# VectorE's signed step tied, by issue order, behind a residual sum written ahead of it

## The chip, the cores and the metric

The kernel runs on one core of a Trainium2 chip. The metric is the device time of one execution in microseconds (us), taken as the median of several runs. The profile shows five engines and the queues that issue DMAs: PE is TensorE (PEld its weight loads), DVE is VectorE, ACT is ScalarE, POOL is GpSimd, SP is SyncE, whose queue issues most transfers here.

## What is computed

Four layers run one after the other on x of 4 batches x 64 channels x 256 x 256 in float32. Layers 0, 1 and 3 are long convolutions with a filter that a small network produces; the filter is a product of a row part and a column part, so the two-dimensional convolution splits into two products with Toeplitz matrices:

```python
k_f = jnp.fft.rfft2(k, s=(fft_size, fft_size)) / fft_size
u_f = jnp.fft.rfft2(x.astype(jnp.float32), s=(fft_size, fft_size))
y = jnp.fft.irfft2(u_f * k_f, s=(fft_size, fft_size))[..., :L, :L]
out = y + x * bias[:, None, None]
```

Layer 2 is a Haar transform, a mixing of the channels with a soft threshold at each coefficient, twice, and the inverse transform:

```python
f1 = haar2d(x)
acc = jnp.zeros_like(f1[:, :conv_w.shape[1]])
for i in range(v.shape[0]):
    f3 = f1 * v[i]
    f4 = jnp.einsum('bchw,oc->bohw', f3, conv_w[i])
    f5 = jnp.sign(f4) * jax.nn.relu(jnp.abs(f4) - tau[i])
    acc = acc + f5
y = haar2d(acc, inverse=True)
return y + x
```

## The kernel before

The work is staged by batch. `convolutions(b)` takes the 64 channels of a batch through layers 0 and 1 and the forward Haar transform and stores the coefficients in DRAM. `mixing(b)` takes the coefficients back in 64 groups g, mixes the channels and thresholds. `inverse(b)` transforms back channel by channel and applies layer 3. While batch b is mixed, batch b + 1 is convolved; the last mixing (b = 3) has layer 3 of some put-off channels beside it instead.

One channel c of a convolution passes through these steps. PE multiplies the input with the layer's Toeplitz matrix into a PSUM bank (`pa0`), ACT copies it out (`a0`, L275), PE multiplies again (`py0`), and VectorE forms the residual sum `y0` = x * bias + py0 (L292, `residual`, shown as y<-x,bsb,py in the profile). That is the first layer. The second does the same from `y0` to `y1` (`pa1`, `a1`, `py1`, then y<-y,bsb,py). After it come `sums` and `sd` (L337, L338), levels of the transform (L350, L351), a split into two parts (`sp`, L369 on ACT, L374 on VectorE), a product on PE (`pz`) and a copy and store (`co`, L393).

One group g of a mixing passes through these: four products on PE into `px` (L449); a scaling of part of it on VectorE (L468) and of the rest on ACT, in up to 12 small steps (L473), both into the tile `f4`; `mag` = |f4| on ACT (L477); the sign of `f4`, in place, on ACT (L480); `shrink`, mag minus the threshold, on VectorE (L484); `signed`, max(mag, 0) times the sign, on VectorE (L488, shown as mag<-mag,f); and `add`, two additions into the large tile `z` (L494). The tiles `f4` and `mag` have two buffers each, and `px` two. The buffer of `f4` comes free after `signed`, that of `mag` after `add`, that of `px` after the ACT steps of L473. Level steps on `z` (`halve`, L299 and L300) undo the transform along one axis as soon as enough of `z` is there.

The order is made in two steps. First the program lists every stage of every unit with a time, counted in ticks, from the table `PLACE`, and writes the instructions in the order of these times. In the first three mixings `signed` of group g stands at tick g + 2.802, and the residual sum of a channel at its own tick + 2.571; 64 channels are spread over some 70 ticks. Then the scheduler of the framework, when it compiles, goes through the instructions in the written order as priority, and puts an instruction into its engine's queue when, by its reckoning, its inputs and a buffer are ready. So an instruction that is ready early can overtake what was written before it. After that each engine's order is fixed and every engine works its queue off in order. A dependency of the kind `order` (no synchronisation) ties one instruction behind another in the queue, and adds no semaphore wait.

```python
order = mybir.DependencyInfo(mybir.DependencyClass.NoSync, mybir.DependencyReason.DATA)
```

The kernel before uses it at a few places of its beginning, where the filters are made.

Of the kernel before, what the change touches and what calls it, by code (L numbers as in the profile page):

```python
# [12 lines left out]
ALU = mybir.AluOpType  # L13
# [3 lines left out]
B, C, S, EMB, ORD = 4, 64, 256, 33, 64  # L17
# [80 lines left out]
def conv_seq_kernel(ctx, tc, x, fz, fw, bias, decay, haar, haar_row, factors, vt, taut, wmix, out):  # L98
# [14 lines left out]
    nc = tc.nc  # L113
# [19 lines left out]
    bsb = const.tile([P, 3, C], F32, name="bsb")  # L133
# [24 lines left out]
    order = mybir.DependencyInfo(mybir.DependencyClass.NoSync, mybir.DependencyReason.DATA)  # L158
# [90 lines left out]
    def toeplitz(layer, c, name):  # L249

        t = tp.tile([P, 2, S], F32, name=name, tag="toep")
        nc.sync.dma_start(t, ap(pads[layer], c * 2 * ROW, [[1, P], [ROW, 2], [1, S]]))
        return t

    def bank(name):
        return psm.tile([P, 2, S], F32, name=name, tag="mm")

    def contract(ps, src, t):

        for m in range(2):  # L260
            nc.tensor.matmul(ps[:, m, :], src[:, 0, m * P : (m + 1) * P], t[:, ::-1], start=True, stop=False)  # L261
            nc.tensor.matmul(ps[:, m, P:], src[:, 1, m * P : (m + 1) * P], t[:, : P - 1 : -1], start=False, stop=True)  # L262
# [16 lines left out]
    def second(b, st, key, layer, res, new, tag, ahead=None):  # L279


        def product(c):
            s = st[c]
            if ahead is not None:
                s[ahead] = toeplitz(ahead, c, f"t{ahead}_{b}_{c}")
            s["p" + new] = bank(f"p{new}_{b}_{c}")
            contract(s["p" + new], s[key], s[layer][:, 1, :])

        def residual(c):
            s = st[c]  # L290
            y = io.tile([P, 2, S], F32, name=f"{new}_{b}_{c}", tag=tag, bufs=BUFS[tag])
            nc.vector.scalar_tensor_tensor(y, s[res], bsb[:, layer, c : c + 1], s["p" + new], ALU.mult, ALU.add)  # L292
            s[new] = y

        return [product, residual]

    def halve(even, odd):

        nc.vector.tensor_sub(odd, even, odd)  # L299
        nc.vector.scalar_tensor_tensor(even, even, 2.0, odd, ALU.mult, ALU.subtract)  # L300

    def level(n, chunk, begin=0, count=None):

        count = n if count is None else count
        v = z.rearrange("p n s x c -> p n s (x c)")[:, chunk].rearrange("p (j e s) x -> p j e s x", e=2, s=P // 2 // n)
        halve(v[:, begin : begin + count, 0, 0, :], v[:, begin : begin + count, 1, 0, :])

    def butterfly():

# [9 lines left out]
    def at(time, run, unit):  # L319
        events.append((time, len(events), run, unit))  # L320
# [104 lines left out]
    def mixing(b, start, n_act):  # L425

        st = {}

        def load(g):
            f = mx.tile([P, 2, S], F32, name=f"f_{b}_{g}", tag="f", bufs=3)  # L430
            nc.sync.dma_start(f, coef[b].rearrange("k c p w -> (k c) p w")[:, 2 * g : 2 * g + 2])
            st[g] = {"f": f}
            if g % GT == 0:
                t = mx.tile([P, 2, GT, 16], F32, name=f"vt_{b}_{g}", tag="vt")
                nc.sync.dma_start(t, scales[g // GT])
                st["vt", g // GT] = t

        def scale(g, i):
            return st["vt", g // GT][:, i, g % GT, :]

        def over(g, i, n):
            return scale(g, i)[:, :n].unsqueeze(2).to_broadcast([P, n, C])

        def mix(g):
            f = st[g]["f"]
            ps = psx.tile([P, 2, 2, S], F32, name=f"px_{b}_{g}", tag="mix")
            for q in range(2):
                for h in range(2):
                    nc.tensor.matmul(  # L449
                        ps[:, q, h, :],  # L450
                        f[:, q, h * P : (h + 1) * P],
                        wb.rearrange("p r n -> p (r n)"),
                        start=True,
                        stop=True,
                    )
            if g == 0:

                one, two = ps[:, 0, :, :P], ps[:, 0, :, P:]
                d = mx.tile([P, 2, P], F32, name=f"d_{b}", tag="mag")
                nc.vector.tensor_copy(d, two)  # L460
                nc.vector.tensor_sub(two, one, d)
                nc.vector.tensor_add(one, one, d)
            st[g]["f4"] = mx.tile([P, 16, C], F32, name=f"f4_{b}_{g}", tag="f4")
            st[g]["px"] = ps.rearrange("p q h (r i o) -> p (q h r i) o", r=2, i=2)

        def scaled(g):
            px, n = st[g]["px"], 16 - n_act
            nc.vector.tensor_tensor(st[g]["f4"][:, :n], px[:, :n], over(g, 0, n), ALU.mult)  # L468

        def scaled_too(g, half):  # L470
            px, f4 = st[g]["px"], st[g]["f4"]
            for j in range(16 - n_act + half * (n_act // 2), 16 - (1 - half) * (n_act - n_act // 2)):
                nc.scalar.mul(f4[:, j], px[:, j], scale(g, 0)[:, j : j + 1])  # L473

        def size(g):
            mag = st[g]["mag"] = mx.tile([P, 16, C], F32, name=f"mag_{b}_{g}", tag="mag")
            nc.scalar.activation(mag, st[g]["f4"], AF.Abs)  # L477

        def sign(g):
            nc.scalar.activation(st[g]["f4"], st[g]["f4"], AF.Sign)  # L480

        def shrink(g):
            mag = st[g]["mag"]
            nc.vector.tensor_sub(mag, mag, over(g, 1, 16))  # L484

        def signed(g):
            mag = st[g]["mag"]
            nc.vector.scalar_tensor_tensor(mag, mag, 0.0, st[g]["f4"], ALU.max, ALU.mult)  # L488

        def add(g):  # L490
            parts = st.pop(g)["mag"].rearrange("p (q x i) (n c) -> p q i x n c", q=2, i=2, n=4)
            for q in range(2):
                to = slot(2 * g + q)
                nc.vector.tensor_add(  # L494
                    z[:, :, to].rearrange("p n x c -> p x n c"), parts[:, q, 0], parts[:, q, 1]
                )


        for g in range(S // 4):
            for name, stage in zip(  # L500
                ("mix load", "mix", "scaled", "scaled too", "scaled rest", "size", "sign", "shrink", "signed", "add"),
                (
                    load,
                    mix,
                    scaled,
                    lambda g: scaled_too(g, 0),
                    lambda g: scaled_too(g, 1),
                    size,
                    sign,
                    shrink,  # L510
                    signed,
                    add,
                ),
            ):
                at(start + g + PLACE[name if b + 1 < B else "l " + name], stage, g)

    def inverse(b, start, put_off):

        st = {}
# [40 lines left out]
        def join(c):  # L560
            ps = st[c]["pw"]
            t = io.tile([P, 2, 2, P], F32, name=f"t_{b}_{c}", tag="res", bufs=BUFS["res"])
            nc.vector.scalar_tensor_tensor(t, st[c]["r"], 0.5, ps, ALU.mult, ALU.add)
            u = io.tile([P, 2, S], F32, name=f"u_{b}_{c}", tag="y", bufs=BUFS["y"])
            v = u.rearrange("p m (w e) -> p m w e", e=2)
            nc.vector.tensor_add(v[:, :, :, 0], t[:, 0], t[:, 1])
            nc.vector.tensor_sub(v[:, :, :, 1], t[:, 0], t[:, 1])
            st[c]["u"] = u
# [20 lines left out]
        for c in range(C):  # L589
            for name, stage in zip(("sooner", "early", "fetch", "rows"), (sooner, early, fetch, rows)):  # L590
                at(start + c + PLACE[name], stage, c)
            turn = start + c
            if c < 16:
                at(start + c + PLACE["halves"], halves, c)
                at(start + c + PLACE["cols"], cols, c)
                turn += 1
            at(turn + PLACE["join"], join, c)
            if c in put_off:
                at(turn + PLACE["aside"], aside, c)
            else:  # L600
                shift = (0.0, 0.0)
                if put_off:
                    shift = ((-0.27, -0.342), (0.23, 0.158))[c % 3]
                for name, stage in zip(("a3", "a3 copy", "y3", "y3 sum", "out"), last(b, st)):
                    at(turn + PLACE[name] + shift[name[0] != "a"], stage, c)
# [59 lines left out]
    ahead = C  # L665
    start = ready + 3
    for b in range(B):
# [11 lines left out]
        ahead = start - 3  # L679
# [4 lines left out]
def slot(i):  # L684

    if i == 0:
        return 0
    n = 1 << i.bit_length() - 1
    return (2 * (i - n) + 1) * (P // 2 // n)
# [104 lines left out]
```

## Time and profile before

| what | us |
|---|---|
| median of 3 runs | 2876.38 |
| lowest and highest | 2875.58 and 2878.57 |
| the profiled execution's own time | 2874.07 |
| its span in the profile | 2872.3 |
| mixing 0, with its beginning | 448 to 856 |
| mixing 1, with its beginning | 1064 to 1510 |
| mixing 2, with its beginning | 1714 to 2158 |
| last mixing | 2358 to 2640 |

The stages between these are the inverse transforms; the first 448 us are the filters and the first batch's convolutions. Times in the lines of a profile are counted from the start of the span. A busy table by stage has, in each row, the stretch and its length, then busy us and number of instructions of PE, PEld, DVE, ACT and POOL, the share of the granted TensorE clock, the share of the DMA engines and GB/s. A line of waits has the engine that waited and for which tile and line, what released it, and us in total, times, and the longest. A line of the timeline has the start, the us, the engine, the line, the operation, out<-in, and how many were merged.

### The profile page before, as it was taken

To read this page: it belongs to the slowest core of one execution; us is meant where nothing else is said; L and a number is where in the kernel's file an instruction comes from. 1 tells how busy PE (TensorE), PEld (TensorE's weight loads), DVE (VectorE), ACT (ScalarE), POOL (GpSimd) and SP (SyncE) were. 2 spreads that over 40 slices of the span, in tenths; PEclk is the share of its full clock that TensorE was granted. 3 is DMA by queue.
4 is the path that set the end of the run, shared out by engine and by line. 5 is a ranking of instruction groups with operands and counts; after the bars stand their busy time and mean duration, and the time that the engine had idled before them with its cause. 6 is when DMAs were issued, how large, how long until landed. Compare 5 with 4: busy or idle time off the path is not lost. (4 is left out here: it accounts for less than half of the span.)

```text
span 2872.3 us, 52434 instructions
## 1 busy us (share of the span) xinstructions
PE 2827.1 (98%) x16592; PEld 2555.6 (89%) x16592; DVE 2494.9 (87%) x4255; ACT 2080.3 (72%) x4950; POOL 334.4 (12%) x644
## 2 busy tenths in 40 slices
PE   9999999999999999999999999999999999999999
PEld 7899998898888898998898998998898998888998
DVE  4655558999999779999999779999999779999985
ACT  2333338999995558998985658999995659998554
POOL 0111111121121001221221001121121000000000
PEclk9999999999999999999999999999999999999999
DMA  6878787776667986777777986777777988787786
GB/s 182 249 231 230 232 232 227 207 208 204 205 209 213 289 254 198 214 213 214 209 207 236 299 255 196 213 214 216 208 208 235 297 266 235 229 238 212 224 241 201
DMA packets 599367, 649.77 MB, mean 226 GB/s; under 512 B 48465, under 2 KB 517044, under 8 KB 598964
## 3 DMA queue, kind: packets, MB, share of 16 engines
q1 hardware_dynamic: 536996, 578.61, 68.9%
q10 hardware_dynamic: 62096, 67.82, 6.7%
q8 instruction: 134, 2.20, 0.3%
q14 instruction: 141, 1.16, 0.1%
HBM read 426.77 MB, written 219.48 MB: 225 GB/s over the span
## 5 line engine op out<-in xcount | busy, mean ns | idle before, releaser
L261 PE MATMUL py<-t,a 128*128 128x256 f32 x3072 | 922.5, 382 | 9.5 <-ACT a L275 8.7
L275 ACT COPY a<-pa 128x512 f32<-128x512 f32 x768 | 478.8, 623 | 498.6 <-PE pa L262 455.2
L473 ACT ACTIVATE f<-px,vt 128x64 f32<-128x64 f32 x2816 | 610.5, 367 | 101.6 <-DVE f L468 101.1
L262 PEld LDWEIGHTS py<-t,a 128*128 128x128 f32 x3072 | 583.4, 190 | 79.3
L262 PE MATMUL py<-t,a 128*128 128x128 f32 x3072 | 590.0, 274 | 0.0
L261 PEld LDWEIGHTS py<-t,a 128*128 128x128 f32 x3072 | 497.3, 191 | 51.2 <-ACT a L275 19.0
L449 PE MATMUL px<-wb,f 128*128 128x256 f32 x2048 | 487.6, 380 | 7.6 <-ACT f L473 7.6
L449 PEld LDWEIGHTS px<-wb,f 128*128 128x128 f32 x2048 | 369.0, 190 | 50.0 <-ACT f L473 10.5
L351 POOL TENSOR_TENSOR sd<-less 128x128 f32<-128x128 f32 (+4 forms) x320 | 190.8, 596 | 1858.7 <-DVE less L350 1519.9
L534 ACT COPY zc<-z 128x512 f32<-128x512 f32 x256 | 282.1, 1105 | 108.1 <-PE pw L542 99.0
L484 DVE TENSOR_TENSOR mag<-mag,vt 128x1024 f32<-128x1024 f32 x256 | 316.6, 1237 | 12.3 <-ACT mag L477 11.5
L488 DVE SCALAR_TENSOR_TENSOR mag<-mag,f 128x1024 f32<-128x1024 f32 x256 | 316.6, 1238 | 0.0
L261 PE MATMUL pa<-t,y 128*128 128x256 f32 x1024 | 309.1, 384 | 6.8 <-DVE y L292 5.2
L261 PE MATMUL pa<-t,x 128*128 128x256 f32 x1024 | 305.9, 381 | 0.5 <-DMA t<-pad 0.5
L477 ACT ACTIVATE mag<-f 128x1024 f32<-128x1024 f32 x256 | 295.7, 1155 | 2.8 <-DVE z L494 0.4
L374 DVE TENSOR_TENSOR sp<-sd,sp 128x512 fp32r<-128x512 f32 x256 | 179.8, 702 | 129.3 <-ACT sp L369 128.2
L480 ACT ACTIVATE f<-f 128x1024 f32<-128x1024 f32 x256 | 285.8, 1116 | 3.5
L261 PE MATMUL pa<-t,u 128*128 128x256 f32 x772 | 233.2, 384 | 6.5 <-ACT w L548 2.8
L292 DVE SCALAR_TENSOR_TENSOR y<-x,bsb,py 128x512 f32<-128x512 f32 x256 | 190.9, 746 | 41.9 <-PE py L262 41.0
L262 PEld LDWEIGHTS pa<-t,x 128*128 128x128 f32 x1024 | 194.6, 190 | 26.3
L262 PEld LDWEIGHTS pa<-t,y 128*128 128x128 f32 x1024 | 194.5, 190 | 26.3
L292 DVE SCALAR_TENSOR_TENSOR y<-y,bsb,py 128x512 f32<-128x512 f32 x256 | 190.7, 745 | 26.0 <-PE py L262 25.6
(73 smaller groups left out, 4412.3 us busy)
## 6 DMA issues: line engine op xcount, KB each, us to landing
t<-pad SPq DMA_DIRECT2D x768, 256.0 KB, 4.1
x<-in_x SPq DMA_DIRECT2D x256, 256.0 KB, 3.7
coef<-co SPq DMA_DIRECT2D x256, 256.0 KB, 3.2
f<-coef SPq DMA_DIRECT2D x256, 256.0 KB, 3.2
r<-keep SPq DMA_DIRECT2D x256, 256.0 KB, 4.1
out_y<-y ACTq DMA_DIRECT2D x193, 256.0 KB, 4.3
keep<-sums SPq DMA_DIRECT2D x256, 128.0 KB, 2.8
keep<-sd SPq DMA_DIRECT2D x256, 128.0 KB, 2.8
```

What stands on the lines that cost most here:

```text
L261: nc.tensor.matmul(ps[:, m, :], src[:, 0, m * P : (m + 1) * P], t[:, ::-1], start=True, stop=False)
L262: nc.tensor.matmul(ps[:, m, P:], src[:, 1, m * P : (m + 1) * P], t[:, : P - 1 : -1], start=False, stop=True)
L275: nc.scalar.copy(a, s["p" + new])
L292: nc.vector.scalar_tensor_tensor(y, s[res], bsb[:, layer, c : c + 1], s["p" + new], ALU.mult, ALU.add)
L351: engine.tensor_tensor(t[:, :, :, half:length], v[..., 0], v[..., 1], ALU.subtract)
L449: nc.tensor.matmul(ps[:, q, h, :], f[:, q, h * P : (h + 1) * P], wb.rearrange("p r n -> p (r n)"), start=True, stop=True,)
L473: nc.scalar.mul(f4[:, j], px[:, j], scale(g, 0)[:, j : j + 1])
L477: nc.scalar.activation(mag, st[g]["f4"], AF.Abs)
L480: nc.scalar.activation(st[g]["f4"], st[g]["f4"], AF.Sign)
L484: nc.vector.tensor_sub(mag, mag, over(g, 1, 16))
L488: nc.vector.scalar_tensor_tensor(mag, mag, 0.0, st[g]["f4"], ALU.max, ALU.mult)
L534: nc.scalar.copy(a.rearrange("p h k i -> p (h k) i"), z[:, c // 16, :, :, c % 16].rearrange("p i x -> p x i"))
```

## The change

A variable `behind` holds the instruction that was written last among the residual sums of the first layer (`y0`) and the joins of the inverse transform (`join`, L563). In the first three mixings each `signed` step gets a dependency of the kind `order` on it. `halve` and `level` get a parameter `stay` with a dependency of the same kind, but no call sets it, so it has no effect.

```diff
+    behind = [None]
...
-            nc.vector.scalar_tensor_tensor(y, s[res], bsb[:, layer, c : c + 1], s["p" + new], ALU.mult, ALU.add)
+            done = nc.vector.scalar_tensor_tensor(y, s[res], bsb[:, layer, c : c + 1], s["p" + new], ALU.mult, ALU.add)
+            if new == "y0":
+                behind[0] = done
             s[new] = y
...
-    def halve(even, odd):
-
-        nc.vector.tensor_sub(odd, even, odd)
+    def halve(even, odd, stay=False):
+
+        first = nc.vector.tensor_sub(odd, even, odd)
+        if stay and behind[0] is not None:
+            tc.add_manual_dep(first.ins, behind[0].ins.name, order, reason="not ahead of the joins")
         nc.vector.scalar_tensor_tensor(even, even, 2.0, odd, ALU.mult, ALU.subtract)
...
         def signed(g):
             mag = st[g]["mag"]
-            nc.vector.scalar_tensor_tensor(mag, mag, 0.0, st[g]["f4"], ALU.max, ALU.mult)
+            step = nc.vector.scalar_tensor_tensor(mag, mag, 0.0, st[g]["f4"], ALU.max, ALU.mult)
+            if b + 1 < B and behind[0] is not None:
+                tc.add_manual_dep(step.ins, behind[0].ins.name, order, reason="the residual sum goes first")
...
         def join(c):
             ps = st[c]["pw"]
             t = io.tile([P, 2, 2, P], F32, name=f"t_{b}_{c}", tag="res", bufs=BUFS["res"])
-            nc.vector.scalar_tensor_tensor(t, st[c]["r"], 0.5, ps, ALU.mult, ALU.add)
+            behind[0] = nc.vector.scalar_tensor_tensor(t, st[c]["r"], 0.5, ps, ALU.mult, ALU.add)
```

More of the change, by code (lines that the diff above doesn't have):

```diff
@@ L291, in residual, with level @@
             y = io.tile([P, 2, S], F32, name=f"{new}_{b}_{c}", tag=tag, bufs=BUFS[tag])
-            nc.vector.scalar_tensor_tensor(y, s[res], bsb[:, layer, c : c + 1], s["p" + new], ALU.mult, ALU.add)
+            done = nc.vector.scalar_tensor_tensor(y, s[res], bsb[:, layer, c : c + 1], s["p" + new], ALU.mult, ALU.add)
+            if new == "y0":
+                behind[0] = done
             s[new] = y
         return [product, residual]
-    def halve(even, odd):
-        nc.vector.tensor_sub(odd, even, odd)
+    def halve(even, odd, stay=False):
+        first = nc.vector.tensor_sub(odd, even, odd)
+        if stay and behind[0] is not None:
+            tc.add_manual_dep(first.ins, behind[0].ins.name, order, reason="not ahead of the joins")
         nc.vector.scalar_tensor_tensor(even, even, 2.0, odd, ALU.mult, ALU.subtract)
-    def level(n, chunk, begin=0, count=None):
+    def level(n, chunk, begin=0, count=None, stay=False):
         count = n if count is None else count
         v = z.rearrange("p n s x c -> p n s (x c)")[:, chunk].rearrange("p (j e s) x -> p j e s x", e=2, s=P // 2 // n)
-        halve(v[:, begin : begin + count, 0, 0, :], v[:, begin : begin + count, 1, 0, :])
+        halve(v[:, begin : begin + count, 0, 0, :], v[:, begin : begin + count, 1, 0, :], stay)
     def butterfly():
```

## The prediction, made before the result was known

> **What bounds the kernel now.** I read the page's busy shares first, then busy time by stage, then what TensorE (PE) waited for in the mixings, then one tick on VectorE (DVE) and ScalarE (ACT).
>
> ```profile
> PE 2827.1 (98%) x16592; PEld 2555.6 (89%) x16592; DVE 2494.9 (87%) x4255; ACT 2080.3 (72%) x4950; POOL 334.4 (12%) x644
> ```
>
> PE is idle for 2872.3 - 2827.1 = 45.2 us of the whole span. The change touches only mixings 0 to 2, so the stages come next (start:end, length, then busy us by engine).
>
> ```profile
> 515.00:856.00 341.00, 335.37 (x1856) 299.02 (x1855) 336.13 (x551) 319.16 (x913) 70.69 (x107) 1.00 0.70 207
> 1130.00:1510.00 380.00, 378.70 (x2126) 341.01 (x2125) 376.71 (x613) 343.62 (x959) 77.87 (x120) 1.00 0.73 212
> ...
> 515.00:666.00 151.00, 149.69 (x828) 133.53 (x827) 149.52 (x248) 144.28 (x415) 29.36 (x47) 1.00 0.71 209
> 666.00:856.00 190.00, 185.67 (x1029) 165.49 (x1029) 186.61 (x304) 174.88 (x500) 41.32 (x60) 1.00 0.69 206
> ```
>
> In mixing 1 PE idles 1.30 of 380 us and DVE 3.29: PE sets the pace, DVE just keeps up. Mixing 2 is its copy (376.73 of 378). Mixing 0 idles 5.63 of 341, 4.33 of it in its second part. The starts of mixings 1 and 2 (66 us each) add 0.92 each and the start of mixing 0 0.06, so all PE idle in the three mixings is 5.69 + 2.22 + 2.19 = 10.1 us. What ended it, mixing 0 first, then mixing 1:
>
> ```profile
> PE py L261 <- ACT a L275: 3.1, 5, 1.4
> PE px L449 <- ACT f L473: 1.4, 2, 1.1
> PE pa L261 <- DVE y L292: 1.0, 3, 0.5
> ...
> PE pa L261 <- DVE y L292: 0.5, 3, 0.2
> PE py L261 <- ACT a L275: 0.5, 1, 0.5
> ```
>
> The residual sum is the smaller part; the copy `a` on ACT is the larger. Now a tick of mixing 1, DVE and then ACT:
>
> ```profile
> 1148.94 1.24 DVE L488 SCALAR_TENSOR_TENSOR mag<-mag,f 128x1024 f32<-128x1024 f32 x1
> 1150.07 0.77 DVE L292 SCALAR_TENSOR_TENSOR y<-x,bsb,py 128x512 f32<-128x512 f32 x1
> 1150.73 0.78 DVE L494 TENSOR_TENSOR z<-mag 128x256 f32<-128x256 f32 x2
> ```
>
> ```profile
> 1149.08 2.56 ACT L473 ACTIVATE f<-px,vt 128x64 f32<-128x64 f32 x12 [0.84 <-DVE f L468]
> 1151.45 0.67 ACT L275 COPY a<-pa 128x512 f32<-128x512 f32 x1
> ...
> 1152.91 1.17 ACT L477 ACTIVATE mag<-f 128x1024 f32<-128x1024 f32 x1
> 1154.11 1.06 ACT L480 ACTIVATE f<-f 128x1024 f32<-128x1024 f32 x1
> 1155.08 0.57 ACT L275 COPY a<-pa 128x512 f32<-128x512 f32 x1
> ```
>
> The reader is to see two things. VectorE's order is not the written order: the signed step at 1148.94 (group 11) runs ahead of the sum `y0` of channel 12 at 1150.07, and group 10's ran at 1141.9, though channel 12's sum is written ahead of both. And ACT has a queue in which `f`, `mag`, sign and the copies `a` stand behind each other.
>
> **The change part by part.** It adds and removes no instruction and no DMA: 192 signed steps (start to next start 1.13 us) stay, each tied by issue order alone. Matching the n-th instruction of each line in the trace with the n-th written, 180 of the 192 now run ahead of the sum they will be tied to (54, 63, 63 by mixing), always a `y0`, never a join. From a signed step's start now to the issue of what follows that sum is in the median 5.2 us in mixing 0 and 7.0 us in 1 and 2. So DVE's busy sum is unchanged, and the signed step moves by about one tick (7.4 us). SP's and POOL's queues hold nothing of it: the loads `f<-coef` wait for the mix matmuls, not for the signed step. What follows:
>
> *A, the sum comes earlier.* A signed step no longer stands just ahead of a `y0`. That is worth at most PE's waits on DVE `y` over the five windows of the three mixings, 1.0 + 0.9 + 0.5 + 0.9 + 0.4 = 3.7 us, and at least nothing, as level steps of the same 1.2 us (L299, L300) can stand there instead. I take -1.9, half, as both rows look alike.
>
> *B, the buffers.* `f4` and `mag` have two buffers each. The scaling of group g+2 (L468) writes the `f4` that signed(g) frees. That slack (end of signed(g) to start of scaled(g+2)) is in the median 2.4 us in mixing 0 and 4.1 in 1 and 2. Tied, signed(g) overruns it at 46, 53 and 53 groups, by about 3.3 us each. That makes `f` late, and PE's `px` two groups later waits for that PSUM buffer; the spare time there is in the median 5.8 us in mixing 0 and 8.2 in the others. Group by group, one step ahead, only one place overruns (group 41 of mixing 0: push 1.2, spare 0.1): +1.1 us. Bounds 0 and, without that cover, 152 x 3.3 = 502 us; I take 1.1, the row by row result.
>
> *C, the queue on ACT.* In the tick above: `y0` at 1150.07, the tied signed(10) at 1150.73, scaled(12) 1.13 later at 1151.86 for 0.42, `f` from about 1152.4 for 2.56, then 1.20 and 0.97 start to start for `mag` and sign, so the copy `a` of the second product (1155.08 now) can start at about 1157.1: 2.0 us late. Its own slack before `py` needs it is in the median 2.4 us in mixings 1 and 2 and 1.4 to 1.5 in mixing 0. The cover is nearly used up; 0.4 us is left, less than mixing 0 has today. How PE fares with less slack is read from mixing 0: its first part idles 1.31 of 151 us (0.87%), its second 4.33 of 190 (2.28%). Mixings 1 and 2, 446 us with their starts, idle 2.2 each; at 2.28% it would be 10.2, so +8.0 each, and mixing 0's 341 us at that rate 7.8, so +2.1: high end +18. Low end 0, if the copies are issued ahead of `mag` in the new order. I take +9.0, the middle: the second layer's copy loses its slack, the first layer's (2.8 us) does not.
>
> *D, the ends.* The last signed step of mixing 1 (1505.85) would follow the sum at 1508.92, at 1509.58: 3.7 us late. It is hidden: the first `zc` copy then starts near 1514.9 instead of 1511.22, and its `pw` on PE stands at 1521.36, behind convolution work. Cost 0; with the cover gone 3.7 + 3.7 + 1.1 (mixing 0, through its buffer) = 8.5.
>
> Sum: -1.9 + 1.1 + 9.0 + 0 = +8.2. The profiled execution took 2874.07 (span 2872.3 and 1.8 around it), 2.3 below the median 2876.38; 2872.3 + 8.2 + 1.8 + 2.3 = **2884.6 us**.
>
> A rule that bears on this: the Trainium skill, Perfetto Trace Analysis, "Identifying the Most-Contended Engine", takes matmul busy time as a poor measure, reads PE by its weight loads and the other engines by occupancy. By it DVE (376.71 of 380 us) leads in mixing 1 and PE's weight loads fill only 341.01; then a mere reordering of DVE's unchanged work is worth nothing, or what DVE idles more, and the sum would be about 2876. The rows of waits, which my sum goes by, show PE without gaps there.
>
> **The rivals.**
>
> 1. *Faster: the sum goes first and the first products follow sooner.* For it: PE's `pa` after a `y0` has in the median only 1.0 us of slack, 0.1 at the least, and the transition after mixing 0 idles 8.13 of 208 us against 2.24 of 204 after mixing 1, so there is something to regain. Against it: 3.7 us is all that the sum costs. If mixing 0 fell to mixing 1's rate (1.30 / 380 x 341 = 1.2) that is -4.4, and the other four windows' waits -2.7: -7.1, with a share of the transition's 5.9 perhaps -8: 2868.4 us. It decides if ACT's copies are issued ahead of the late `f`.
>
> 2. *No change: the cover holds.* Only A and B act: -1.9 + 1.1 = -0.8, 2875.6 us. For it: 8.2 us of spare time for `px`, an order laid out anew around the later step. Against it: the 0.4 us left in C.
>
> 3. *Much slower.* If the copies `co` and the cast `sp` (0.47 and 0.52 start to start) stand ahead of `a` too, it is 2.0 + 1.0 - 2.4 = 0.6 us late in each of 106 groups of mixings 1 and 2: +64, 2940 us.
>
> 4. *It doesn't do what it says:* the order stays, 2876. Against it: 180 steps stand on the wrong side of the tie and must move.
>
> **How the numbers follow.** A measurement of this kernel tells 0.2%, 5.75 us, from no change. The forecast has 0.43, rival 1 0.25, rival 2 with 4 0.27, rival 3 0.05. So faster by over 0.2% 0.25, within 0.2% 0.27, slower 0.48. The forecast's own range is 2882 to 2894 (C at 7 to 18). The range that should hold 8 in 10 runs from 2868, where about half of rival 1 lies below, to 2900, which leaves out rival 3 and a little of the forecast.
>
> **What would show it.** In the changed kernel's trace each `mag<-mag,f` step of mixings 0 to 2 stands behind its `y0`; if many still precede it, the premise fails. A: the waits PE `pa` <- DVE `y` in mixings 0 to 2 fall below 3.7. B: `px` <- ACT `f` stays near 1.4 there. C: PE `py` <- ACT `a` rises from 4.1 over the three mixings to about 13, and the copy starts some 2 us later after `pa`. If C's waits stay at 4 and the time does not rise, C is wrong and rival 2 or 1 holds; if the loss stands after 856, 1510 and 2158 us instead, D's cover was missing.

## The result, and the profile after

| | before | after |
|---|---|---|
| median, us | 2876.4 | 2896.45 |
| lowest to highest, us | 2875.58 to 2878.57 | 2893.52 to 2897.42 |
| the profiled execution's own time, us | 2874.07 | 2896.96 |
| its span, us | 2872.3 | 2895.0 |
| idle time of PE in the span, us | 45.2 | 57.9 |

The changed kernel takes 1.0071 times as long (95% interval 1.006 to 1.0082): 20 us are lost. The prediction had 2884.6 and 2868 to 2900, so the sign and the range held. The loss was about two and a half times its +8.2, and the time lies above the 2882 to 2894 that it gave the forecast itself. Lines of code from L263 on stand two to eight further down than before: the residual sum is L294, the copy `a` L277, the products `px` L455, the scaling L474, ACT's scaling `f` L479, `mag` L483, the sign L486, `shrink` L490, `signed` L494, `zc` L542.

First the busy line of the page of the changed kernel, then its busy table by stage (mixing 0 and mixing 1 after their starts, then two parts of mixing 0; columns as in the table of before).

```profile
PE 2837.1 (98%) x16592; PEld 2556.2 (88%) x16592; DVE 2501.0 (86%) x4255; ACT 2085.9 (72%) x4950; POOL 343.6 (12%) x644
```

```profile
515.00:873.00 358.00, 341.35 (x1856) 302.84 (x1855) 348.88 (x563) 322.77 (x925) 63.67 (x110) 0.99 0.67 198
...
1143.00:1527.00 384.00, 379.99 (x2119) 339.34 (x2118) 379.00 (x612) 347.77 (x971) 90.33 (x127) 1.00 0.71 209
...
690.00:710.00 20.00, 16.53 (x83) 14.48 (x82) 14.53 (x25) 14.52 (x44) 6.63 (x9) 0.91 0.49 150
860.00:873.00 13.00, 9.74 (x47) 8.51 (x47) 12.94 (x21) 9.53 (x24) 0.00 (x0) 0.87 0.68 182
```

Mixing 0's main part is 358 us long where it was 341, with the same 1856 matmuls. PE idles 358 - 341.35 = 16.65 us of it, where it idled 5.63: 11.0 of the 17 us are open gaps. The other 6.0 sit in PE's busy time, which rises from 335.37 to 341.35 for the same matmuls; in the whole span it rises by 10.0. Part of the 6.0 is the clock: the granted share is 0.99 in this row and 1.00 in that of before. It is 0.91 from 690 to 710 us and 0.87 from 860 to 873, each time behind a long wait of PE (3.5 and 2.6 us, both shown further down), and 1.00 in the rest of it; 20 x 0.09 + 13 x 0.13 is some 3.5 us, an estimate. Mixing 1 idles 4.01 of 384, where it idled 1.30 of 380.

Where the loss arises is read by taking the same event in both traces and subtracting. The end of the last `px` of mixing 0 comes 14.5 us later than before; 1.3 of that is regained by the end of the inverse transform (13.2). Mixing 1 adds 3.9 up to its last `px`, and its inverse another 1.6 (18.7). Mixing 2 adds 3.7 and 0.4 (22.8). After that nothing changes. So about two thirds of the loss belong to mixing 0, and within it the products `px` of groups 16, 32 and 48 start 1.4, 4.8 and 11.5 us later than before: it grows with the groups and is not a cost of the ends.

What PE waited for in the changed kernel, mixing 0 first (448 to 873 us), then mixing 1 (1077 to 1527; columns as before, us in total, times, longest):

```profile
PE px L455 <- ACT f L479: 8.8, 14, 1.5
PE py L263 <- ACT a L277: 6.9, 4, 3.5
PE pz L387 <- ACT sp L375: 0.9, 3, 0.5
...
PE px L455 <- ACT f L479: 1.7, 3, 0.6
PE py L263 <- ACT a L277: 1.4, 4, 0.5
PE pz L387 <- DVE y L294: 0.5, 1, 0.5
...
PEld py L263 <- ACT a L277: 5.1, 10, 0.9
PEld px L455 <- ACT f L479: 2.9, 5, 0.8
```

The row that the change was aimed at, `pa` <- DVE `y`, is gone from PE in all three mixings (`pz` <- DVE `y`, 0.5 us in each of mixings 1 and 2, is new). In its place stands `px` <- ACT `f`: 1.4 us over the three mixings before, 8.8 + 1.7 + 1.7 = 12.2 now. The copy `a` went from 4.1 to 6.9 + 1.4 + 1.1 = 9.4. In mixing 1 the weight loads (PEld) wait longer than the matmuls, 8.0 us in these two rows against 3.1, so here a late weight load doesn't show as a gap of the same size between the matmuls.

One case of the main row, from the timeline of the changed kernel in mixing 0 (start, us, engine, line, operation). It is the buffer of group 32.

```profile
653.99 0.60 PE L455 MATMUL px<-wb,f 128*128 128x256 f32 x2
...
655.93 0.75 DVE L294 SCALAR_TENSOR_TENSOR y<-x,bsb,py 128x512 f32<-128x512 f32 x1
656.60 1.22 DVE L494 SCALAR_TENSOR_TENSOR mag<-mag,f 128x1024 f32<-128x1024 f32 x1
...
658.39 0.42 DVE L474 TENSOR_TENSOR f<-px,vt 128x256 f32<-128x256 f32 x1
...
659.03 1.17 ACT L486 ACTIVATE f<-f 128x1024 f32<-128x1024 f32 x1
659.99 2.67 ACT L479 ACTIVATE f<-px,vt 128x64 f32<-128x64 f32 x12
...
662.72 0.48 PE L455 MATMUL px<-wb,f 128*128 128x256 f32 x1 [0.70 <-ACT f L479]
```

The products of group 32 end at 654.59, so their scaling could start. It writes the `f4` that group 30's signed step frees, and that step, tied, waits for the sum at 655.93 and ends at 657.82. The scaling runs at 658.39, 3.8 us late; ACT's `f` follows the sign at 659.99 and ends at 662.66; and PE, which needs the same PSUM bank for group 34, stands still until 662.72. In the trace of before signed(30) had ended 2.25 us before the products of group 32 did, and the bank had 4.21 us to spare.

Over all groups, medians in us:

| from, to | mixing 0 before | after | mixings 1, 2 before | after |
|---|---|---|---|---|
| `shrink` end to `signed` start | 0.9 | 4.0 | 1.0 | 5.6 |
| `px` end to scaling start | 0.8 | 4.9 | 0.8 | 5.4 |
| `f4` free to the scaling two groups on | 2.4 | 0.6 | 4.2 | 0.6 |
| `f` end to `px` two groups on (spare of the bank) | 5.8 | 1.0 | 8.3 | 3.3 |
| `mag` free to `mag` two groups on | 2.4 | 2.2 | 4.7 | 2.0 |

No signed step of the three mixings runs ahead of its sum any more (180 did). The buffer of `f4` now decides when nearly every scaling starts (within 1.5 us of its coming free at 182 of 186 groups, at 29 before), and the spare of the bank is what paid for it: under 0.3 us is left at 20 of 62 groups of mixing 0, where it was smaller (at 2 before), and at 7 each in the other two, where more than half of it is gone. How long `f4` is held, from the start of its scaling to the end of `signed`, tells the mixings apart. In the median it was 9.9 us in mixing 0 and 9.7 in the others, and is 12.8 and 13.5 now. Two buffers cover two groups, and two groups took 12.6 us in mixing 0 of before and 13.8 in the others (mean distance of `px`, twice): the hold is now beyond that in mixing 0 and just below it in the other two.

### The profile page after: what moved, and what is told of

It is laid out like the page before. It is cut to its first block, busy times and chain, and to the rows that moved or that the text cites. A ratio compares the mean times of both kernels' runs of the same rounds, so it can differ in the third digit from the quotient of the medians.

```text
span 2895.0 us, 52539 instructions
## 1 busy us (share of the span) xinstructions
PE 2837.1 (98%) x16592; PEld 2556.2 (88%) x16592; DVE 2501.0 (86%) x4255; ACT 2085.9 (72%) x4950; POOL 343.6 (12%) x644
## 5 line engine op out<-in xcount | busy, mean ns | idle before, releaser
L263 PE MATMUL py<-t,a 128*128 128x256 f32 x3072 | 925.3, 383 | 16.5 <-ACT a L277 15.4
L277 ACT COPY a<-pa 128x512 f32<-128x512 f32 x768 | 480.2, 625 | 535.0 <-PE pa L264 490.6
L479 ACT ACTIVATE f<-px,vt 128x64 f32<-128x64 f32 x2816 | 618.2, 387 | 76.0 <-DVE f L474 74.9
L263 PEld LDWEIGHTS py<-t,a 128*128 128x128 f32 x3072 | 497.1, 191 | 62.1 <-ACT a L277 31.4
L455 PE MATMUL px<-wb,f 128*128 128x256 f32 x2048 | 495.2, 382 | 18.9 <-ACT f L479 18.3
L455 PEld LDWEIGHTS px<-wb,f 128*128 128x128 f32 x2048 | 367.3, 190 | 65.3 <-ACT f L479 26.7
L357 POOL TENSOR_TENSOR sd<-less 128x128 f32<-128x128 f32 (+4 forms) x320 | 182.4, 570 | 1843.9 <-DVE less L356 1717.8
L542 ACT COPY zc<-z 128x512 f32<-128x512 f32 x256 | 281.9, 1104 | 105.6 <-PE pw L550 95.2
L490 DVE TENSOR_TENSOR mag<-mag,vt 128x1024 f32<-128x1024 f32 x256 | 313.6, 1225 | 17.8 <-ACT mag L483 17.1
L494 DVE SCALAR_TENSOR_TENSOR mag<-mag,f 128x1024 f32<-128x1024 f32 x256 | 312.8, 1222 | 0.0
L263 PE MATMUL pa<-t,y 128*128 128x256 f32 x1024 | 308.0, 383 | 2.2 <-DMA t<-pad 2.0
L263 PE MATMUL pa<-t,x 128*128 128x256 f32 x1024 | 305.9, 381 | 0.6 <-DMA t<-pad 0.6
L483 ACT ACTIVATE mag<-f 128x1024 f32<-128x1024 f32 x256 | 296.0, 1156 | 3.4 <-ACT f L479 0.2
L486 ACT ACTIVATE f<-f 128x1024 f32<-128x1024 f32 x256 | 289.0, 1129 | 3.0
L294 DVE SCALAR_TENSOR_TENSOR y<-x,bsb,py 128x512 f32<-128x512 f32 x256 | 190.2, 743 | 55.1 <-PE py L264 53.5
L263 PE MATMUL pa<-t,u 128*128 128x256 f32 x772 | 231.8, 382 | 4.5 <-DVE u L575 2.0
L294 DVE SCALAR_TENSOR_TENSOR y<-y,bsb,py 128x512 f32<-128x512 f32 x256 | 189.5, 740 | 16.8 <-PE py L264 16.6
```

What stands on the lines that cost most here:

```text
L277: nc.scalar.copy(a, s["p" + new])
L294: done = nc.vector.scalar_tensor_tensor(y, s[res], bsb[:, layer, c : c + 1], s["p" + new], ALU.mult, ALU.add)
L357: engine.tensor_tensor(t[:, :, :, half:length], v[..., 0], v[..., 1], ALU.subtract)
L455: nc.tensor.matmul(ps[:, q, h, :], f[:, q, h * P : (h + 1) * P], wb.rearrange("p r n -> p (r n)"), start=True, stop=True,)
L494: step = nc.vector.scalar_tensor_tensor(mag, mag, 0.0, st[g]["f4"], ALU.max, ALU.mult)
L542: nc.scalar.copy(a.rearrange("p h k i -> p (h k) i"), z[:, c // 16, :, :, c % 16].rearrange("p i x -> p x i"))
```

## The experiments

A loss in us behind a ratio is the ratio less 1, times the time of before; the difference of the two medians can be up to 3 us off it. Each profile is one execution.

**Which mixing.** Two kernels tie only some of the mixings. In this and all later diffs `...` stands for lines left out; with more buffers of a tile these are the same edit at the other tiles that share its buffers.

```diff
-            if b + 1 < B and behind[0] is not None:
+            if b == 0 and behind[0] is not None:
```

> The tie in mixing 0 alone. Buffer theory (a late signed step frees f4 late, so scaling, f on ACT and the px bank are late, and PE's next px waits): mixing 0 has the least spare time before px (median 0.9 us with the tie, against 3.3 in mixings 1 and 2), so it carries most: +13 to +18 us over the kernel before, with PE px <- ACT f near 9 us there. Queue theory (step C of the forecast, the copies a behind the late f, mag and sign): mixing 0 was put at +2.1, so +1 to +5. Reshuffle theory (any new tie upsets the whole order, no single path): anything between 0 and +23, with no relation to the px waits.

Measured: 2890.82 us beside 2874.67 of before, ratio 1.0047 (1.0031 to 1.0062), +13.5 us. In its profile 15.9 us arise between the first and the last `px` of mixing 0 and nothing is added later (the first `px` is already 4.5 us later than before, ahead of any tie).

```diff
-            if b + 1 < B and behind[0] is not None:
+            if 0 < b < B - 1 and behind[0] is not None:
```

> The tie in mixings 1 and 2 alone. Buffer theory: spare time before px stays at 3.3 us in the median, so only +7 to +11 us over the kernel before, the rest to the 20 us of the change. Queue theory: +16, most of the whole. Reshuffle theory: this and the tie in mixing 0 alone need not add up to the change.

Measured: 2885.52 us beside the same 2874.67, ratio 1.0036 (1.0024 to 1.0048), +10.3 us; in its profile 5 to 6 us in each of the two. The two parts make 24, the change 20; with intervals of about 4 us each they add up. Both lie where the buffer theory had them, and the queue theory has them the wrong way round. That mixing 0, with the least spare time, carries more than the other two together isn't certain from the times; in the profiles it is 15.9 us against 8.8 (first to last `px`).

**How far behind.** The signed step is tied behind the sum or join written one earlier.

```diff
-    behind = [None]
+    behind = [None, None]
...
-                behind[0] = done
+                behind[:] = [done, behind[0]]
...
-            if b + 1 < B and behind[0] is not None:
-                tc.add_manual_dep(step.ins, behind[0].ins.name, order, reason="the residual sum goes first")
+            if b + 1 < B and behind[1] is not None:
+                tc.add_manual_dep(step.ins, behind[1].ins.name, order, reason="the residual sum goes first")
...
-            behind[0] = nc.vector.scalar_tensor_tensor(t, st[c]["r"], 0.5, ps, ALU.mult, ALU.add)
+            behind[:] = [nc.vector.scalar_tensor_tensor(t, st[c]["r"], 0.5, ps, ALU.mult, ALU.add), behind[0]]
```

> The same tie, but behind the sum or join written one earlier than the last. The signed step is then no later than some 0 to 2 us after its place in the kernel before (7.0 us late less one channel of 7.4 in mixings 1 and 2, 5.2 less some 8 in mixing 0). Buffer theory and queue theory: the loss goes, -4 to +3 us against the kernel before. Reshuffle theory: still +5 to +20, since there are as many ties.

Measured: 2873.72 us, ratio 0.9992 (0.9983 to 1.0001): no difference. Only 37 of the 192 ties move anything here, by 1.1 to 2.8 us. So 192 ties that move little cost nothing; in the change `signed` starts 6.4 and 8.0 us later behind its group's `px` (mixing 0, and 1 and 2), about a tick. As most of the order stays as it was, this run doesn't yet rule out the reshuffle theory; the kernels with third buffers do.

**Which buffer.** The tie is put on other steps of the same group: first on `add`, so that `f4` is freed as before and only `mag` is held longer.

```diff
-            if b + 1 < B and behind[0] is not None:
-                tc.add_manual_dep(step.ins, behind[0].ins.name, order, reason="the residual sum goes first")
...
-                nc.vector.tensor_add(
+                step = nc.vector.tensor_add(
                     z[:, :, to].rearrange("p n x c -> p x n c"), parts[:, q, 0], parts[:, q, 1]
                 )
+                if b + 1 < B and behind[0] is not None:
+                    tc.add_manual_dep(step.ins, behind[0].ins.name, order, reason="the residual sum goes first")
```

> The addition into z is tied behind the same sum, and the signed step is free. The buffer of mag is then held for as long as with the change, that of f4 is not. Buffer theory by f4: the loss goes, -3 to +5 us against the kernel before. If the buffer of mag is the path, or DVE's place in the order behind PE as such: +15 to +23. Queue theory: mag and sign on ACT are not late for want of f4, so 0 to +6.

Measured: 2883.97 us, ratio 1.0029 (1.002 to 1.0038), +8.3 us, between the ranges of the theories and in none. PE's waits in the whole span of this kernel:

```profile
PE py L263 <- ACT a L277: 12.5, 24, 1.3
PE pw L549 <- ACT zc L542: 8.0, 5, 2.5
PE px L455 <- ACT f L479: 6.7, 7, 1.3
```

The row of `px` is below the 7.6 us that it has in the whole trace of before, and the spare of its bank is nearly what it was (5.3 and 8.1 us in the median): with `f4` free in time that route is closed. 8 us are still lost, but not in the mixings. `mag` is held 11.1 and 12.6 us, as long as in the change (11.0 and 12.1), and has 1.5 and 1.4 us left from free to use (2.4 and 4.7 before). Yet from the first to the last `px` the three mixings change by -0.4, +0.8 and +0.8 us against before. The loss of this profile (9.3 us) stands elsewhere: 3.9 us ahead of the first `px`, where the order is that of before, so not by the tie, and 3.5 and 2.8 us in the inverse transforms after mixings 1 and 2. There PE waits for `zc`, up to 2.5 us at a time (the row went from 2.0 to 8.0); `zc` reads the `z` that the tied additions write and takes `mag`'s buffers, but no run shows which of the two holds it up, or whether something else does. So a `mag` that is held a tick longer costs the mixings next to nothing by itself while it isn't taken the moment it comes free.

Then the tie is put on the scaling itself, with the signed step free.

```diff
-            nc.vector.tensor_tensor(st[g]["f4"][:, :n], px[:, :n], over(g, 0, n), ALU.mult)
+            step = nc.vector.tensor_tensor(st[g]["f4"][:, :n], px[:, :n], over(g, 0, n), ALU.mult)
+            if b + 1 < B and behind[0] is not None:
+                tc.add_manual_dep(step.ins, behind[0].ins.name, order, reason="the residual sum goes first")
...
-            if b + 1 < B and behind[0] is not None:
-                tc.add_manual_dep(step.ins, behind[0].ins.name, order, reason="the residual sum goes first")
```

> The scaling on VectorE (the first instruction that writes f4) is tied behind the same sums, the signed step is free. f4 and mag are given back as early as in the kernel before, but the scaling of group g+2 starts no earlier than behind the sum that held it back with the change. If the loss comes by late scaling, late f and a late px bank: +14 to +22 us, with PE px <- ACT f near the 12.2 us of the change's three mixings. If it comes by the buffer of mag (the tied addition alone cost 8 to 9) or by the signed step's own place: +0 to +6. Reshuffle theory: +8 to +22 with no rise of px <- ACT f.

Measured: 2881.57 us beside 2876.7, ratio 1.0014 (1.0004 to 1.0023), +4.0 us: a miss. The reason is in its trace: the scaling follows the sum directly, not the sum and then the signed step, and starts 2.5 and 2.8 us after `px`, where the change has 4.9 and 5.4; the bank keeps 5.0 and 6.6 us to spare. It was less than half the dose (1.7 and 2.0 us later than before, where the change has 4.1 and 4.6). The row it raised is the expected one:

```profile
PE px L455 <- ACT f L481: 12.5, 17, 1.3
```

12.5 us in the whole span, 7.6 before and 18.3 in the change.

**A third buffer for one of the two.** The space comes from two of the six Toeplitz tiles, so each needs a control. First the change with three `f4`:

```diff
-    tp = ctx.enter_context(tc.tile_pool(name="toep", bufs=6))
+    tp = ctx.enter_context(tc.tile_pool(name="toep", bufs=4))
...
-            st[g]["f4"] = mx.tile([P, 16, C], F32, name=f"f4_{b}_{g}", tag="f4")
+            st[g]["f4"] = mx.tile([P, 16, C], F32, name=f"f4_{b}_{g}", tag="f4", bufs=3)
...
```

> The change with three buffers of f4 instead of two, and four instead of six Toeplitz tiles to make room. To be compared with the same buffers without the tie. Buffer theory by f4: the late signed step no longer holds back the next scaling but one, so the tie costs only what the buffer of mag costs, +4 to +9 us over the kernel without the tie, and PE px <- ACT f in mixings 0 to 2 falls from 12.2 to under 4. Queue and reshuffle theories: the tie still costs +15 to +22.

Measured: 2949.96 us, ratio 1.0255 (1.024 to 1.0271). The control has the same two edits on the kernel before, without the tie:

> The kernel before with three buffers of f4 and four Toeplitz tiles, no tie: the control. f4 seldom held PE up in the kernel before (px <- ACT f 1.4 us in mixings 0 to 2), so all theories: -4 to +2 us from f4, plus what two Toeplitz tiles fewer cost, 0 to +10.

Measured: 2932.0 us, ratio 1.0195 (1.018 to 1.0211), some 56 us where 12 at most had been expected. The largest of PE's waits in it is for the Toeplitz tiles:

```profile
PE pa L261 <- DMA t<-pad: 36.2, 26, 4.1
```

That row had 1.5 us before. The granted clock is lower too, 0.994 where before has 0.999; 0.5% of the span is some 15 us, an estimate. The tie costs 2949.96 - 2932.0 = 18 us on top (at a clock of 0.993), almost as much as with two buffers; in the profiles 15.5 us of it arise between the first and the last `px` of the three mixings. So `f4` alone, by which +4 to +9 had been expected, is not the whole of it. `f4` no longer decides (the scaling starts 0.8 and 0.9 us after `px`, as before the change, and the bank has its 5.0 and 8.3 us). `mag` does: ACT takes its buffer at most 0.3 us after it comes free at 35, 48 and 48 groups of the three mixings, where the kernel with the tied additions has 2, 6 and 6. Then the change with three `mag` and two `f4`:

```diff
-            mag = st[g]["mag"] = mx.tile([P, 16, C], F32, name=f"mag_{b}_{g}", tag="mag")
+            mag = st[g]["mag"] = mx.tile([P, 16, C], F32, name=f"mag_{b}_{g}", tag="mag", bufs=3)
...
```

> The change with three buffers of mag instead of two, two of f4, and four Toeplitz tiles. Buffer theory by f4: the greater part stays, +10 to +18 us over the control without the tie. If mag is the main path: +0 to +6 over that control, and PE py <- ACT a falls back towards the level of the kernel before.

Measured: 2952.82 us, ratio 1.0269 (1.0251 to 1.0286), 21 us over the same control (which has three `f4`, so the comparison is not exact), a little more than either theory gave. `f4` decides as in the change: 0.6 us from free to use, 1.1 and 3.4 us left of the bank. One more buffer of either alone moves the wait to the other.

**A third buffer for both.** The space is taken where it costs less: one Toeplitz tile, two of five `y`, one of three `co`.

```diff
-BUFS = {"res": 1, "y": 5, "co": 3}
+BUFS = {"res": 1, "y": 3, "co": 2}
...
-    tp = ctx.enter_context(tc.tile_pool(name="toep", bufs=6))
+    tp = ctx.enter_context(tc.tile_pool(name="toep", bufs=5))
...
-            st[g]["f4"] = mx.tile([P, 16, C], F32, name=f"f4_{b}_{g}", tag="f4")
+            st[g]["f4"] = mx.tile([P, 16, C], F32, name=f"f4_{b}_{g}", tag="f4", bufs=3)
...
-            mag = st[g]["mag"] = mx.tile([P, 16, C], F32, name=f"mag_{b}_{g}", tag="mag")
+            mag = st[g]["mag"] = mx.tile([P, 16, C], F32, name=f"mag_{b}_{g}", tag="mag", bufs=3)
...
```

With the tie:

> The change with three buffers of f4 and three of mag; room for them comes from five Toeplitz tiles instead of six, three of y instead of five and two of co instead of three. To be compared with the same buffers without the tie. Buffer theory: a signed step one tick late no longer holds back scaling or mag two groups on, so the tie costs nothing or gains what the sums cost: -6 to +5 us over that control, px <- ACT f in the mixings as in the control. Reshuffle theory: the tie costs +12 to +24 over the control as it did with two buffers (+20), with f4 alone at three (+18) and mag alone at three (+21).

Measured: 2912.27 us beside 2877.31, ratio 1.0123 (1.0105 to 1.014). The control, the same without the tie:

> The control: the kernel before with three buffers of f4 and mag and the same cuts of the other tiles, no tie. f4 and mag seldom held it up, so what it loses is the cost of the cuts: 0 to +60 us over the kernel before, by all theories.

Measured: 2914.68 us, ratio 1.0135 (1.0115 to 1.0155). The tie costs 2912.27 - 2914.68 = -2.4 us here; the two ratios differ by -0.0012 with some 0.0027 (8 us) either way, which leaves out +20 us. All 192 signed steps stand behind their sums in the tied kernel, and later than in the change (6.4 and 8.3 us after `shrink`). What the view of waits lists for PE in mixing 0 (448 to 873 us), with the tie and then without it:

```profile
PE pa L263 <- DVE y L294: 1.9, 5, 0.7
PE py L263 <- ACT a L277: 1.3, 2, 1.0
PE pa L263 <- DMA t<-pad: 1.0, 1, 1.0
```

```profile
PE py L261 <- ACT a L275: 1.6, 4, 1.0
PE pa L261 <- DVE y L292: 1.5, 4, 0.5
PE pa L261 <- DVE sp L374: 0.4, 1, 0.4
```

`px` <- ACT `f`, 8.8 us in the change, is in neither. The scaling starts 1.0 and 0.9 us after `px`, the bank has 5.7 and 8.4 us. From the first to the last `px` neither kernel loses more than 0.3 us in any of the three mixings against before, so what the smaller pools cost (38 us) lies outside the mixings and doesn't hide the tie's price there. The same order of sum and signed step, with a third buffer of each, is free within these 8 us: the loss of the change comes by the time for which the two buffers of `f4` and of `mag` are held, first `f4`, and `mag` as soon as `f4` has a third.

**One wait of another kind.** The largest single wait of mixing 0, 3.5 us, is not `px`. From the timeline of the changed kernel:

```profile
696.50 0.20 POOL L357 TENSOR_TENSOR sd<-less 128x8 f32<-128x8 f32 x1
696.74 0.62 ACT L375 CAST sp<-sd 128x512 fp32r<-128x512 f32 x1 [5.37 <-POOL sd L357]
697.26 0.58 ACT L277 COPY a<-pa 128x512 f32<-128x512 f32 x1
...
697.90 1.22 PE L263 MATMUL py<-t,a 128*128 128x256 f32 x2 [3.47 <-ACT a L277]
```

The `py` pair at 697.90 takes 1.22 us, where a pair of that shape takes 0.60 (the `px` at 653.99 above): the granted clock is 0.57 from 698 to 701.5 us. In the new order ACT's queue comes to the cast `sp` of a channel before GpSimd's small levels for it are done, and the copy `a` stands behind the cast for 5.4 us. Over the span this wait of the cast rose from 8.1 to 17.2 us. To see what it is worth, the ties of groups 34 to 37 of mixing 0 are lifted, and in a control those of groups 44 to 47, which lie behind it.

```diff
-            if b + 1 < B and behind[0] is not None:
+            if b + 1 < B and not (b == 0 and 34 <= g <= 37) and behind[0] is not None:
```

> In the change, group 34's to 37's ties of mixing 0 are lifted, 188 ties stay. In the changed kernel's trace one wait of PE there (py on the copy a, 3.5 us near 697.9) stands behind ScalarE's cast sp, which waits 5.4 us for GpSimd's small levels. Theory A (that wait is a single event of the new order beside the buffer loss): with the ties lifted the cast waits under 2.5 us there, PE's 3.5 us wait is gone, and the time is 3 to 5 us below the change, about 2892 beside a before of 2876.4. Theory B (the wait only takes over lateness that px would pay anyway): the wait is gone or not, but the loss by the end of px of group 63 stays within 1.5 us of the change's +14.5, and the time stays within 1.5 us of 2896.5.

Measured: 2895.99 us beside 2875.35, ratio 1.007 (1.0057 to 1.0084). What ACT waited for from 640 to 720 us, and then PE in mixing 0:

```profile
ACT sp L375 <- POOL sd L357: 2.9, 1, 2.9
...
PE px L455 <- ACT f L479: 10.1, 13, 2.5
PE py L263 <- ACT a L277: 3.8, 4, 2.5
```

The cast's wait falls from 5.4 to 2.9 us but isn't gone. PE's wait on `a` behind it is (6.9 to 3.8 in mixing 0), and `px` has taken its place (8.8 to 10.1): PE now stands 2.5 us there for an `f` that follows the cast in ACT's queue, with no pause of ACT in between. `pa` <- DVE `y` is back at 2.3. The last `px` of mixing 0 stands at +15.9 against the change's +14.5. The control:

```diff
-            if b + 1 < B and behind[0] is not None:
+            if b + 1 < B and not (b == 0 and 44 <= g <= 47) and behind[0] is not None:
```

> In the change, the ties of groups 44 to 47 of mixing 0 are lifted instead; the order up to there, with the 3.5 us wait near 697.9, stays as in the change. Both theories: PE's wait of about 3.5 us and the cast's of about 5.4 us stay; four groups of 64 lifted give back about 4/64 of mixing 0's 14.5 us, some 1 us, so 2894 to 2897 beside a before of 2876.4. Below 2893 would mean that any change of the order in mixing 0 moves the time by as much as theory A claims for the one wait.

Measured: 2896.24 us, ratio 1.0075 (1.0062 to 1.0088), and the 5.4 and 3.4 us waits are where they were. The largest single wait is gone in the first of the two and the time has not moved: the 3 to 5 us of theory A didn't come. But its condition, a cast that waits under 2.5 us, wasn't met either, so what the cast's wait is worth stays open. What the pair shows is that the same lateness was paid at `px` in place of `py`: the rows of waits tell where it is paid, not who owes it.

No version beat both kernels. Not tried: third buffers without taking space from other tiles, and a kernel that delays only ACT's copies `a`.

## Why the prediction was right, and where it was wrong

The sign and the range held, but the mechanism that was to carry the loss was not the one that did. The forecast put +9.0 on ACT's copies (C) and +1.1 on the buffers (B). That the time fell within 2868 to 2900 is in part luck: the upper bound was set for C, and it left room for B's error. The prediction's own signs say so: `px` <- ACT `f`, which was to stay near 1.4, reads 12.2, and `py` <- ACT `a`, which was to reach about 13, reads 9.4.

**The premise** held: all 192 signed steps stand behind their sums, and DVE's busy time hardly changed (2494.9 to 2501.0).

**A, the sum comes earlier (-1.9).** The wait went, and to the full bound: `pa` <- DVE `y`, 3.7 us over the three mixings, left PE's rows altogether. By that it was under-sized by 1.9, on the side that would have made the total smaller; what it was worth in time no run shows by itself.

**B, the buffers (+1.1).** This is the step that failed. The route was named in full (late signed, late scaling, late `f`, `px` waits for its bank), but its size came from "group by group, one step ahead": each group's push of about 3.3 us was set against that group's spare time in the old trace, and only one place overran. Measured, the scaling is 4.1 to 4.6 us later, the spare time falls from 5.8 to 1.0 and from 8.3 to 3.3 us and is used up at 20 groups of mixing 0, not at one, and PE's row rises by 10.8 us, that of the weight loads by 16.3 (2.2 to 18.5). Part of it is the push itself, 4.1 to 4.6 us where 3.3 were reckoned. The rest fits with a lateness that returns: a late `px` and `f` are followed by late work on the same three engines, so the next group starts with less, which a single step can't see. That return is argued; the experiments show the buffers as the cause by their relief (+20 with two of each, -2.4 us with three), and give no law for the size. B also left out `mag`, which takes over once `f4` is relieved (18 us with three `f4` and two `mag`).

**C, the queue on ACT (+9.0).** The mechanism is there. At the end of mixing 0, in the timeline of the changed kernel:

```profile
862.85 2.72 ACT L479 ACTIVATE f<-px,vt 128x64 f32<-128x64 f32 x12
865.21 0.84 ACT L399 COPY co<-pz 128x512 f32<-128x512 f32 x1
...
865.67 1.33 ACT L483 ACTIVATE mag<-f 128x1024 f32<-128x1024 f32 x1
866.63 0.85 ACT L277 COPY a<-pa 128x512 f32<-128x512 f32 x1
...
867.53 0.70 PE L263 MATMUL py<-t,a 128*128 128x256 f32 x2 [2.56 <-ACT a L277]
```

A late `f` pushes `co`, `mag` and then the copy, and PE waits 2.6 us; behind it is the second stretch of lower clock (0.87 from 860 to 873 us). But where it was placed was wrong: mixings 1 and 2 were given +8.0 each at most and mixing 0 +2.1. They took some 4 to 5 us each, copies and `px` together, and mixing 0 took 13 to 14. PE's row for `a` rose by 5.3, not by about 9, and 3.5 of that is the wait behind the cast `sp`, which the prediction didn't have. In the weight loads the row rose by 11.1 (8.1 to 19.2). So C as a number is near the part that it stood for only if the weight loads are counted, and B should have been the larger term.

**D, the ends (0).** Right for mixings 1 and 2, as worked out: in mixings 1 and 2 the last `add` comes 3.7 us later than the last `px` does, the 3.7 of the prediction, and the first fetch of the inverse transform brings none of it along: its first join stands 0.1 us nearer to before's than the last `px` does. In mixing 0 the last `add` is 2.5 us later than the last `px`, and the first join 1.6. The 1.6 us that the inverse transform after mixing 1 adds arise behind its first join, and no run follows them.

**The rivals.** Rival 1 (faster) had the sum's wait right, which went, and the price wrong; its condition, copies issued ahead of the late `f`, isn't what the trace shows. Rival 2 (the cover holds) took the 8.2 us of spare time as enough; it fell to 3.3 us, and the 5.8 of mixing 0 to 1.0, so that cover is what gave way. Rival 3 (2940) asked for 0.6 us in each of 106 groups of mixings 1 and 2; those mixings lost about 10 us (9.6 in the profile), not 64. Rival 4 falls with the premise.

The prediction weighed a rule of the Trainium skill, Perfetto Trace Analysis, "Identifying the Most-Contended Engine", and drew from it that reordering VectorE's unchanged work would be worth about nothing, 2876 us. The runs don't agree with what was drawn: VectorE's work was only reordered and the kernel lost 20 us, through buffers and not through any engine's load. Another sentence of the same page, under "Optimization Strategy", fits: it takes a gap that repeats on the engine that should be full as a hint at too few buffers. Here the repeating row was `px` <- ACT `f`, 14 times in mixing 0, and third buffers removed it.

## What to carry to other kernels

Before a step is moved later in its queue, list every buffer that it frees and count how many ticks each is held; with two buffers, a hold that the delay brings close to two ticks reaches the producer even when each group seems to have spare time. Don't set such a delay against the spare time of the old trace group by group, one step ahead; that gave +1.1 us here. Carrying the lateness round the loop (sum, signed, scaling, `f`, `px`, next sum) until it settles is the obvious next thing to try, and no run here tests how well it does. To test it, give each held buffer a third copy, all of them at once, with a control that pays the same space: one at a time only moves the wait.

## What the runs showed of the hardware that had not been expected

PE's busy time rose by 10.0 us for the same 16592 matmuls: idle time alone shows 12.7 of the 22.7 us by which the span grew. A wait of PE cost twice here. Behind the waits of 3.5 and 2.6 us in mixing 0 the granted clock fell to 0.57 from 698 to 701.5 us and to 0.87 from 860 to 873, and a matmul pair took 1.22 us in place of 0.60; before has one such stretch, 0.57 from 936 to 940, in the inverse transform. The length of the wait alone doesn't decide it: that stretch follows a wait of 1.9 us, and a wait of 2.0 us at 877 has none behind it. The mean over the span, 0.999 in both, hides all of this. The clock explains some 3.5 of the 6.0 us in mixing 0 and 1.8 of the 10.0 in the whole span, estimates from these shares. Over the three mixings the weight loads' wait for `f` grew from 2.2 to 18.5 us and the matmuls' own from 1.4 to 12.2, which fits with busy time that hides part of a late weight load; no run tested that by itself.

GpSimd's time for one shape, roughly measured as it is by the profile, varies tenfold within a trace: the level 128x64 took 0.29 us at 681.60 and 3.13 us at 641.46 in the trace of before. What stretches it stays open. A cast behind GpSimd in ACT's queue waited up to 5.4 us in the new order and up to 2.3 in the old one.

Two of six Toeplitz tiles fewer, with a third `f4`, cost some 56 us (1.0195), although the loads took about as long to land (4.2 us in the median against 4.1 before): PE's waits for them rose from 1.5 to 36.2 us, and the granted clock fell from 0.999 to 0.994.
